# Square roots by a power operation on GpSimd, and small vector chains moved from VectorE to GpSimd

## The chip, the cores and the metric

The kernel runs on one core of a Trainium2 chip. A core has a matrix engine (TensorE, PE in the profile), a vector engine (VectorE, DVE), a scalar engine (ScalarE, ACT), a general engine (GpSimd, POOL) and an engine that mostly issues transfers (SyncE, SP). Each works through its own queue of instructions in order, and semaphores tie the queues together. The metric is device microseconds of one execution; lower is better.

## The reference, cut to what matters

Two layers work on x (8 batches of 112 rows by 256) with a context of 8 x 375 x 256. All arithmetic is float32.

```python
x = x + L0_xattn(layernorm(x), ctx)           # 16 heads of 16, biases
x = x + L0_ffn(layernorm(x))                  # routed, 8 experts, best 2
x = x + L1_xattn(layernorm(x), ctx, mask)     # additive mask
x = x + L1_ffn(layernorm(x))                  # quantized to ternary weights, depthwise conv, silu
```

with

```python
layernorm(x)  = (x - mean) / sqrt(var + 1e-5)
project(v)    = v * min(1, 0.95 / |v|)                      # into a ball
x_hyper = project(x @ Wp + bp);  c = project(centroids)     # 8 centroids
diff  = max(|x_hyper|^2 + |c|^2 - 2 x_hyper.c, 0)
denom = (1 - |x_hyper|^2)(1 - |c|^2) + 1e-7
dist  = arccosh(max(1 + 2 diff / denom, 1 + 1e-7))
top 2 of -dist, softmax of the two as weights
out   = sum over the two of weight * (gelu(x @ W1[e] + b1[e]) @ W2[e] + b2[e])
```

Square roots are needed in three places: 1/sqrt(var + eps) of each normalization (one number a row), 0.95/|v| of the ball (one number a row, eight for the centroids), and sqrt(m*m - 1) in the softmax of two arccosh values (two numbers a row).

## The kernel before, in words

The eight batches are the unit of work; a tile of one batch has 112 partitions (rows of x) by 256 columns. The program has four stages one after the other.

The first attention (0 to about 297 us) carries a routing pipeline inside it. A plan lists the steps of every batch with a slot (four slots a batch) and a place in the slot: normalize and transpose (`norm`, `t_n`), query, key and value products (`t_q`, `t_k`, `t_v`), scores and their row maxima (`sc`, `top`, L587), the scores turned round with the maximum folded in (`t_p`), exponentials on ScalarE (`pT`), the weighted values (`po`), and the closing steps, of which `project` adds into x and takes the statistics of the new x (`ln_stats`). From slot 4b+13 on come the eight routing steps of batch b: `norm` (writes `rn`) and `turn` (`t_rn`), `hyper` (`t_xh`), `centre` (g, the ball's scale r), `distance` (v), two `pick`s, `place` and `weigh`. `place` works out the row in the scratch tensor `tok` to which each token goes (`at`) and issues two scatters of `rn` from GpSimd's queue (L375). A scatter waits until the one before it has landed, since both write `tok`. `rn` has two buffers, so the normalized row of batch b+2 waits until both scatters of batch b are through. `weigh` works out the two shares. The plan gives the order of priority; the framework then schedules the instructions of each engine by its own cost estimates and sets the semaphores.

The expert stage (297 to 456 us) runs 21 tiles of 128 tokens through the experts' weights, which stream in by transfers from SP's queue; it begins with a load of `tn` from `tok`. The second attention (456 to 701 us) starts each batch with `combine`: two gathers from GpSimd's queue (L510), two weighted additions into x on VectorE (L514), and statistics. Then it is the first attention again, with a mask and without routing: VectorE adds the mask to `pT` (L627). The last stage (701 to 793 us) quantizes, convolves and multiplies, and is mostly VectorE's.

`rsqrt` (L184 to L202) makes a first guess from the exponent bits by a shift and a multiply-add on integers, and improves it by three Newton steps, all on VectorE: nine instructions for one number a row, eleven for more. `ln_stats` (L204), `ball_scale` (L255) and `weigh` (L383) call it. `ln_apply` (L215, its instruction on L217) does the normalization proper, also on VectorE.

Of the kernel before, what the change touches and what calls it, by code (L numbers as in the profile page):

```python
# [54 lines left out]
def xattn_ffn_kernel(  # L55
# [129 lines left out]
    def rsqrt(x, dst, n, name):  # L185


        p = x.shape[0]
        h = sp.tile([p, n], F32, tag=f"{name}h", name="h")
        a = sp.tile([p, n], F32, tag=f"{name}a", name="a")  # L190
        bits = dst.bitcast(I32)
        nc.vector.tensor_scalar(bits, x.bitcast(I32), 1, None, ALU.logical_shift_right)
        nc.vector.tensor_scalar(bits, bits, -1.0, 1597463007.0, ALU.mult, ALU.add)
        if n == 1:
            nc.vector.tensor_scalar_mul(h, x, -0.5)
        for _ in range(3):
            if n == 1:
                nc.vector.scalar_tensor_tensor(a, dst, dst, h, ALU.mult, ALU.mult)  # L198
            else:
                nc.vector.tensor_mul(a, dst, dst)  # L200
                nc.vector.scalar_tensor_tensor(a, a, -0.5, x, ALU.mult, ALU.mult)
            nc.vector.scalar_tensor_tensor(dst, a, 1.5, dst, ALU.add, ALU.mult)  # L202

    def ln_stats(b):  # L204

        st = sp.tile([S, 6], F32, tag="bnst", name="bnst")
        nc.vector.bn_stats(st, xs[b])
        mv = sp.tile([S, 2], F32, tag=f"mv{b}", name="mv")
        nc.vector.bn_aggr(mv, st)
        nc.vector.tensor_scalar_add(mv[:, 1:2], mv[:, 1:2], 1e-5)  # L210
        rs = sp.tile([S, 1], F32, tag=f"rs{b}", name="rs")
        rsqrt(mv[:, 1:2], rs, 1, "ln")
        return mv, rs

    def ln_apply(dst, b, stats):  # L215
        mv, rs = stats
        nc.vector.tensor_scalar(dst, xs[b], mv[:, 0:1], rs, ALU.subtract, ALU.mult)  # L217
# [28 lines left out]
    class Router:  # L246
# [9 lines left out]
        def ball_scale(self, sq, r, n, name):  # L256

            c = self.tmp(f"c{name}", n, sq.shape[0])
            nc.vector.tensor_scalar_max(c, sq, 1e-14)
            rsqrt(c, r, n, f"ball{name}")  # L260
            nc.vector.tensor_scalar(r, r, 0.95, 1.0, ALU.mult, ALU.min)

        def centroids(self):
# [9 lines left out]
            self.ball_scale(self.cn, cs, E, "c")  # L273
# [6 lines left out]
        def norm(self, b, stats):  # L280
            n = self.pool.tile([S, D], F32, tag="r_n", name="rn")
            ln_apply(n, b, stats)
# [25 lines left out]
        def centre(self, xh, xsq):  # L308
# [9 lines left out]
            self.ball_scale(g[:, E : E + 1], r, 1, "x")  # L318
            return g, r

        def distance(self, g, r):

            tmp = self.tmp
            xn = tmp("xn", 1)
            nc.vector.scalar_tensor_tensor(xn, g[:, E : E + 1], r, r, ALU.mult, ALU.mult)
            nc.vector.tensor_scalar_min(xn, xn, 0.99)
            xn1 = tmp("xn1", 1)
            nc.vector.tensor_scalar(xn1, xn, -1.0, 1.0, ALU.mult, ALU.add)
            m2r = tmp("m2r", 1)
            nc.vector.tensor_scalar_mul(m2r, r, -2.0)  # L330

            dif = tmp("dif", E)
            nc.vector.scalar_tensor_tensor(dif, g[:, 0:E], m2r, self.cn[:S], ALU.mult, ALU.add)
            nc.vector.tensor_scalar(dif, dif, xn, 0.0, ALU.add, ALU.max)

            den = tmp("den", E)
            nc.vector.tensor_scalar(den, self.cn1[:S], xn1, 1e-7, ALU.mult, ALU.add)
            nc.vector.reciprocal(den, den)
            nc.vector.scalar_tensor_tensor(dif, dif, 2.0, den, ALU.mult, ALU.mult)
            nc.vector.tensor_scalar(dif, dif, 1.0, 1.0 + 1e-7, ALU.add, ALU.max)  # L340
            v = tmp("v", E)
            nc.vector.tensor_scalar_mul(v, dif, -1.0)
# [17 lines left out]
        def place(self, b, n, ohs):  # L360
# [9 lines left out]
            for k in range(2):  # L370
                nc.vector.tensor_mul(sel[:, k], ohs[k], row)
            nc.vector.tensor_reduce(rf, sel, AX.X, ALU.add)
            nc.vector.tensor_copy(at[b], rf)
# [654 lines left out]
```

## Time and profile before

| | |
|---|---|
| median of 3 runs | 796.31 us (794.44 to 800.98) |
| the profiled execution | 795.12 us, span 793.4 us |
| mean granted PE clock | 0.841 |
| busy: PE, DVE, ACT, POOL | 670.2, 462.1, 240.9, 43.3 us |
| instructions: PE, DVE, POOL | 5906, 1664, 83 |
| DVE rows of the Newton steps on one number of a normalization (L198, L202) | 96 of 219 ns, 96 of 157 ns |
| two-input addition on POOL, 112x256 (L521) | 8 of 726 ns |
| scatter and gather issues on POOL (L375, L510) | 16 of 954 ns, 16 of 937 ns |

A row of the profile names a line of the kernel, the engine, the operation, what is written and read, the shapes, how often, and the busy time with the mean of one. The time after the bar is how long the engine stood idle just before such instructions, and what ended that. A row in order of time begins with its start and its length in us.

### The profile page before, as it was taken

How to read it: one execution, taken by the hardware profiler on the slowest of the kernel's cores; microseconds unless marked ns; L12 is line 12 of the kernel's file. 1: busy time of each engine (PE TensorE's matmuls, PEld its weight loads, DVE VectorE, ACT ScalarE, POOL GpSimd, SP SyncE). 2: the span in 40 equal slices, each digit the busy share in tenths (PEclk: the TensorE clock that was granted, in tenths of full speed). 3: DMA queues.
4: the chain of work that ended last, by engine and by line, in shares of the span. 5: the costliest groups of instructions: out<-in, count | busy, mean ns of one | idle time of the engine just before them, and what ended most of it. 6: DMA issues, size and time to landing. Idle time of an engine off the chain costs nothing.

```text
span 793.4 us, 15060 instructions
## 1 busy us (share of the span) xinstructions
PE 670.2 (84%) x5906; PEld 483.3 (61%) x5906; DVE 462.1 (58%) x1664; ACT 240.9 (30%) x476; POOL 43.3 (5%) x83
## 2 busy tenths in 40 slices
PE   4999998999989819999999968999999989845143
PEld 2666666666656519998999844566666656621033
DVE  8853767766844760111111148759887785569975
ACT  1123342323233204434334310133433322317300
POOL 4000000100000110000000061000000000000000
PEclk9998999989777959999999975579999985556558
DMA  9999101002000115988899420000000000000001
GB/s 309 366 344 321 62 2 54 14 13 68 14 12 8 31 45 206 332 287 327 331 351 344 169 82 19 1 2 1 2 2 2 2 2 1 1 1 0 0 11 35
DMA packets 37074, 82.73 MB, mean 104 GB/s; under 512 B 3228, under 2 KB 29196, under 8 KB 31628
## 3 DMA queue, kind: packets, MB, share of 16 engines
q1 hardware_dynamic: 34092, 76.25, 27.2%
q0 software_dynamic: 1536, 3.67, 1.5%
q10 hardware_dynamic: 1376, 1.87, 0.7%
q8 instruction: 46, 0.75, 0.4%
q14 instruction: 24, 0.20, 0.1%
HBM read 61.59 MB, written 20.19 MB: 103 GB/s over the span
## 4 chain that ended last, share of the span: by engine, by line
PE 68%; DVE 20%; DMA 5%; issue 4%; ACT 3%; POOL 0%; another core or an unknown queue 0%; POOLq 0%; DVEq 0%; ACTq 0%; SPq 0%
PE t_k L229 10%; PE t_h L799 10%; PE t_y L810 9%; PE t_p L617 8%; PE sc L584 7%; PE po L639 6%; PE t_q L534 4%; PE t_v L236 4%; DMA tok<-rn,at 2%; DVE a L198 2%; PE t_out L672 2%; DVE am L924 2%; PE t_o L651 1%; DVE top L587 1%; PE t_y L942 1%
## 5 line engine op out<-in xcount | busy, mean ns | idle before, releaser
L229 PE MATMUL t_k<-ctx,wk 128*128 128x375 f32 x256 | 100.5, 538 | 4.0 <-DMA ctx<-in_ctxT_dram 3.2
L799 PE MATMUL t_h<-tnT,we 128*128 128x128 f32 x672 | 91.4, 280 | 0.6 <-DMA we<-in_WA_dram 0.4
L799 PEld LDWEIGHTS t_h<-tnT,we 128*128 128x128 f32 x672 | 87.1, 193 | 7.5 <-ACT hT L803 1.6
L584 PE MATMUL sc<-k,q 16*112 16x375 f32 x512 | 88.0, 593 | 4.3 <-DVE pT L627 3.2
L803 ACT ACTIVATE hT<-t_h,we 128x128 f32<-128x128 f32 x168 | 61.4, 368 | 91.3 <-PE t_h L799 85.7
L617 PE MATMUL t_p<-qa,k 17*125 17x112 f32 x1536 | 81.9, 323 | 2.4 <-DVE top L587 1.5
L810 PE MATMUL t_y<-we,hT 128*128 128x256 f32 x336 | 82.8, 380 | 0.0
L629 ACT ACTIVATE pT<-pT 125x672 f32<-125x672 f32 x64 | 48.8, 763 | 107.7 <-DVE pT L627 105.5
L617 PEld LDWEIGHTS t_p<-qa,k 17*125 17x125 f32 x1536 | 65.0, 215 | 21.2 <-issue 14.8
L587 DVE TENSOR_REDUCE top<-sc 112x2 f32<-112x750 f32 x64 | 57.9, 935 | 27.2 <-PE sc L584 27.2
L229 PEld LDWEIGHTS t_k<-ctx,wk 128*128 128x128 f32 x256 | 51.1, 211 | 37.1 <-issue 9.7
L627 DVE TENSOR_TENSOR pT<-t_p,maskT 125x336 f32<-125x336 f32 x128 | 56.6, 500 | 24.9 <-PE t_p L617 24.9
L639 PE MATMUL po<-pT,v 125*32 125x112 f32 x1536 | 65.9, 299 | 6.1 <-ACT pT L629 3.7
L629 ACT ACTIVATE pT<-t_p 125x672 f32<-125x672 f32 x64 | 43.3, 728 | 90.7 <-PE t_p L617 90.7
L594 DVE CUSTOM_DVE_ANT_0 sm<-sc,mask 112x375 f32<-112x375 f32 x128 | 63.1, 543 | 9.9 <-PE sc L584 9.9
L639 PEld LDWEIGHTS po<-pT,v 125*32 125x32 f32 x1536 | 43.4, 124 | 31.4 <-ACT pT L629 13.3
L810 PEld LDWEIGHTS t_y<-we,hT 128*128 128x128 f32 x336 | 59.1, 191 | 5.5
L788 DVE COPY tnT<-t_tn 128x256 f32<-128x256 f32 x21 | 8.9, 425 | 77.2 <-PE t_tn L786 70.6
L812 DVE TENSOR_TENSOR y<-t_y,we 128x256 f32<-128x256 f32 x21 | 8.9, 425 | 68.9 <-PE t_y L810 63.9
L584 PEld LDWEIGHTS sc<-k,q 16*112 16x112 f32 x512 | 29.4, 192 | 30.9 <-issue 19.7
L236 PE MATMUL t_v<-wv,ctx 128*125 128x256 f32 x192 | 45.9, 387 | 0.3 <-ACT k L557 0.3
L534 PEld LDWEIGHTS t_q<-nT,wq 128*128 128x128 f32 x256 | 36.2, 225 | 7.5 <-DVE qa L607 3.7
(207 smaller groups left out, 780.6 us busy)
## 6 DMA issues: line engine op xcount, KB each, us to landing
we<-in_WB_dram SPq DMA_DIRECT2D x21, 1152.0 KB, 8.2
we<-in_WA_dram SPq DMA_DIRECT2D x21, 1028.0 KB, 6.5
tok<-zero SPq DMA_DIRECT2D x8, 896.0 KB, 9.7
ysc<-zero SPq DMA_DIRECT2D x8, 896.0 KB, 10.8
ctx<-in_ctxT_dram SPq DMA_DIRECT2D x8, 375.0 KB, 6.5
tn<-tok SPq DMA_DIRECT2D x21, 128.0 KB, 7.4
ysc<-y SPq DMA_DIRECT2D x21, 128.0 KB, 3.3
we<-in_w1T_dram SPq DMA_DIRECT2D x1, 1024.0 KB, 9.4
```

The lines of the kernel that those rows point to most:

```text
L229: nc.tensor.matmul(t, wts[layer]["k"][:, c, g * 128 : (g + 1) * 128], ctx_t[b][:, c, :], start=(c == 0), stop=(c == 1),)
L236: nc.tensor.matmul(t, ctx_t[b][:, c, i * KC : (i + 1) * KC], wts[layer]["v"][:, c, :], start=(c == 0), stop=(c == 1),)
L534: nc.tensor.matmul(t[:, g, :], wts[layer]["q"][:, c, g * 128 : (g + 1) * 128], nT[:, c, :], start=(c == 0), stop=(c == 1),)
L584: nc.tensor.matmul(ts[j // 2][:S, j % 2, :SK], q[r, g, :], k[r, g, :], start=True, stop=True)
L587: nc.vector.tensor_reduce(top[:, g, 2 * m : 2 * m + 2, A : A + 1], ts[m][:S, :, :SK], AX.X, ALU.max, negate=True,)
L594: nc.vector.tensor_tensor_reduce(out=sm, in0=ts[m][:S, i, :SK], in1=mask_t, scale=-1.0, scalar=3.0e38, op0=ALU.add, op1=ALU.min, accum_out ...
L617: nc.tensor.matmul(ts[j // 2][:KC, j % 2, c * S : (c + 1) * S], k[r, g, c * KC : (c + 1) * KC], qa[r, g, :], start=True, stop=True,)
L629: nc.scalar.activation(pT, src, AF.Exp)
L639: nc.tensor.matmul(po[32 * j : 32 * j + 32, g, :], v[:, c, 4 * g + j, :], pTs[j // 2][:, j % 2, c * S : (c + 1) * S], start=(c == 0), stop ...
L799: nc.tensor.matmul(ph[:, i, :], w1[:, c, f * 128 : (f + 1) * 128], nt[:, c, :], start=(c == 0), stop=(c == 1),)
L803: nc.scalar.activation(hT[:, f, :], ph[:, i, :], AF.Gelu, bias=b1[:, f : f + 1])
L810: nc.tensor.matmul(py, hT[:, f, :], w2[:, f, :], start=(f == 0), stop=(f == NF - 1))
```

## The change

`rsqrt` becomes a single GpSimd instruction that raises to the power -0.5, with a constant tile of -0.5 as its second operand. The addition of 1e-5, the scaling of the ball, the whole of `distance` but its reciprocal, the two selections, the integer copy and the running count of `place`, and `weigh` but its reciprocal go to GpSimd with it. So do the routing normalization, and the attentions' normalization of every batch but the first. Where an instruction of VectorE took three operands (a tensor, a column and a second tensor), GpSimd has two instructions in its place. `distance` is put in another order.

```diff
-    def rsqrt(x, dst, n, name):
-        p = x.shape[0]
-        h = sp.tile([p, n], F32, tag=f"{name}h", name="h")
-        a = sp.tile([p, n], F32, tag=f"{name}a", name="a")
-        bits = dst.bitcast(I32)
-        nc.vector.tensor_scalar(bits, x.bitcast(I32), 1, None, ALU.logical_shift_right)
-        nc.vector.tensor_scalar(bits, bits, -1.0, 1597463007.0, ALU.mult, ALU.add)
-        if n == 1:
-            nc.vector.tensor_scalar_mul(h, x, -0.5)
-        for _ in range(3):
...
+    minus_half = const([128, E], "mhalf")
+    nc.gpsimd.memset(minus_half, -0.5)
+
+    def rsqrt(x, dst):
+        nc.gpsimd.tensor_tensor(dst, x, minus_half[: x.shape[0], : x.shape[1]], ALU.pow)
 
     def ln_stats(b):
...
-        nc.vector.tensor_scalar_add(mv[:, 1:2], mv[:, 1:2], 1e-5)
         rs = sp.tile([S, 1], F32, tag=f"rs{b}", name="rs")
-        rsqrt(mv[:, 1:2], rs, 1, "ln")
+        nc.gpsimd.tensor_scalar_add(rs, mv[:, 1:2], 1e-5)
+        rsqrt(rs, rs)
         return mv, rs
 
-    def ln_apply(dst, b, stats):
+    def ln_apply(dst, b, stats, eng=None):
         mv, rs = stats
-        nc.vector.tensor_scalar(dst, xs[b], mv[:, 0:1], rs, ALU.subtract, ALU.mult)
+        (eng or nc.vector).tensor_scalar(dst, xs[b], mv[:, 0:1], rs, ALU.subtract, ALU.mult)
...
         def distance(self, g, r):
...
+            tmp, eng = self.tmp, nc.gpsimd
+            xn, xn1, m2r = tmp("xn", 1), tmp("xn1", 1), tmp("m2r", 1)
+            eng.tensor_scalar(m2r, r, -2.0, None, ALU.mult)
+
+            dif, den = tmp("dif", E), tmp("den", E)
+            eng.tensor_scalar(dif, g[:, 0:E], m2r, None, ALU.mult)
+            eng.tensor_scalar(xn, g[:, E : E + 1], r, r, ALU.mult, ALU.mult)
+            eng.tensor_scalar(xn, xn, 0.99, None, ALU.min)
+            eng.tensor_scalar(xn1, xn, -1.0, 1.0, ALU.mult, ALU.add)
+
+            eng.tensor_scalar(den, self.cn1[:S], xn1, 1e-7, ALU.mult, ALU.add)
             nc.vector.reciprocal(den, den)
+            eng.tensor_add(dif, dif, self.cn[:S])
+            eng.tensor_scalar(dif, dif, xn, 0.0, ALU.add, ALU.max)
+            eng.tensor_mul(dif, dif, den)
+            eng.tensor_scalar(dif, dif, 2.0, 1.0, ALU.mult, ALU.add)
             v = tmp("v", E)
+            eng.tensor_scalar(v, dif, 1.0 + 1e-7, -1.0, ALU.max, ALU.mult)
             return v
...
             for k in range(2):
-                nc.vector.tensor_mul(sel[:, k], ohs[k], row)
+                nc.gpsimd.tensor_mul(sel[:, k], ohs[k], row)
             nc.vector.tensor_reduce(rf, sel, AX.X, ALU.add)
-            nc.vector.tensor_copy(at[b], rf)
+            nc.gpsimd.tensor_copy(at[b], rf)
...
+            nc.gpsimd.tensor_scalar(z, m, 1.0, None, ALU.add)
+            nc.gpsimd.tensor_scalar(q, m, -1.0, None, ALU.add)
+            nc.gpsimd.tensor_mul(z, z, q)
+            rsqrt(z, q)
+            nc.gpsimd.tensor_mul(q, q, z)
+            nc.gpsimd.tensor_sub(u, q, m)
+            nc.gpsimd.tensor_add(r, u[:, 0:1], u[:, 1:2])
             nc.vector.reciprocal(r, r)
+            nc.gpsimd.tensor_scalar(share[b][:, 0:1], u[:, 1:2], r, None, ALU.mult)
+            nc.gpsimd.tensor_scalar(share[b][:, 1:2], u[:, 0:1], r, None, ALU.mult)
...
-                ln_apply(n, b, stats.pop(b))
+                ln_apply(n, b, stats.pop(b), nc.gpsimd if b else nc.vector)
```

## The prediction

> **What bounds the kernel now.** I read the page's busy shares first, then busy time by stretch, then the chain of work that ended last, then single instructions in order of time where TensorE (PE) stood still.
>
> ```profile
> PE 670.2 (84%) x5906; PEld 483.3 (61%) x5906; DVE 462.1 (58%) x1664; ACT 240.9 (30%) x476; POOL 43.3 (5%) x83
> ...
> PE 68%; DVE 20%; DMA 5%; issue 4%; ACT 3%; POOL 0%; another core or an unknown queue 0%; POOLq 0%; DVEq 0%; ACTq 0%; SPq 0%
> ```
>
> PE carries 68% of the chain, VectorE (DVE) 20%, GpSimd (POOL) nothing. An average hides the stages, so here they are (columns: stretch; PE, weight loads, DVE, ACT, POOL busy; granted PE clock; DMA share; GB/s):
>
> ```profile
> 100.00:230.00 130.00, 122.44 (x1335) 84.64 (x1328) 85.80 (x361) 43.19 (x88) 6.55 (x7) 0.87 0.08 25
> 230.00:264.00 34.00, 28.84 (x331) 19.49 (x330) 19.09 (x132) 10.83 (x20) 3.77 (x4) 0.85 0.05 15
> 264.00:297.00 33.00, 15.91 (x85) 12.14 (x83) 22.86 (x174) 4.42 (x12) 5.66 (x6) 0.72 0.13 41
> ...
> 505.00:640.00 135.00, 134.87 (x1531) 87.54 (x1529) 106.29 (x371) 48.09 (x70) 0.00 (x0) 0.93 0.01 2
> 640.00:701.00 61.00, 53.89 (x521) 34.36 (x519) 33.55 (x114) 16.57 (x25) 0.00 (x0) 0.56 0.01 1
> ```
>
> In 100:230 (first attention, with routing) PE is nearly full but not always at full clock; 264:297 is a routing tail in which PE mostly waits; in 640:701 PE is busy at half clock. The waits inside:
>
> ```profile
> 230.43 0.94 POOL L375 DMA_INDIRECT tok<-rn,at  x1 [27.24 <-DVE cx L259]
> 234.07 0.94 POOL L375 DMA_INDIRECT tok<-rn,at  x1 [2.70 <-DMA tok<-rn,at]
> 236.68 0.41 DVE L217 TENSOR_SCALAR rn<-x,mv,rs 112x256 f32<-112x256 f32 x1 [1.30 <-DMA tok<-rn,at]
> 237.24 0.38 PE L288 MATMUL t_rn<-ident,rn 112*128 112x112 f32 x2 [1.43 <-DVE oh L349]
> ...
> 288.38 0.94 POOL L375 DMA_INDIRECT tok<-rn,at  x1 [4.80 <-DVE q L202]
> ...
> 471.08 0.64 PE L524 MATMUL t_n<-ident,n 112*128 112x112 f32 x2 [7.07 <-DVE rs L202]
> ...
> 643.98 0.16 DVE L202 SCALAR_TENSOR_TENSOR rs<-a,rs 112x1 f32<-112x1 f32 x1
> 644.06 1.75 DVE L627 TENSOR_TENSOR pT<-t_p,maskT 125x336 f32<-125x336 f32 x4
> 645.13 0.89 PE L584 MATMUL sc<-k,q 16*112 16x375 f32 x4 [1.62 <-DVE pT L627]
> ```
>
> The second scatter waits for the first to land, the normalized row `rn` two batches on waits for both (two buffers), and PE's `t_rn` waits for `rn`. At 644 us a root on DVE (642.3 to 644.1) holds `pT` up, PE stands 1.62 us, and its clock falls to half.
>
> **What the skill says.** (1) GPSIMD Engine Reference, § 3.1 Elementwise: a two-input f32 add of 2048 columns takes 4497 ns on GpSimd. The trace's only such row is L521, 256 columns, 726 ns; together a slope of 2.1 ns per column and a fixed part of 726 - 256 x 2.1 = 190 ns. The select of masks.py:199 (128 columns, 288 ns), at the memset slope of L157 (1369 / 1536 = 0.9), leaves 177 ns: they agree. (2) Same page, § 2.1 Instruction dispatch: the first call of a freshly loaded GpSimd routine may cost about 6 us; no run here shows it. (3) SBUF — State Buffer, § Who interferes with whom: a DVE instruction with two SBUF inputs blocks against a GpSimd instruction that reads; GpSimd is too idle before to show it. (4) TensorE: Matmul & The Clock Gate, Part 1: an idle window of about 3.4 us halves the clock, and a busy one restores it. The trace agrees on the drop after the 7.07 us gap, but at 644 us it dropped after less, and stayed at 0.50 to 712 us through stretches of full PE: partly.
>
> **The change, part by part.**
>
> *DVE gets lighter.* Per routed batch 55 DVE instructions go: variance and its root 10 (1.68 us busy), ball scale 11 (1.86), distances 10 (1.84), weights 18 (2.96), placing 4 (0.59), the two normalizations 2 (0.87): 9.8 us, from rows such as L198, 20.2 us for 96. Over the kernel, with 24 more roots and the centroids, about 124 of 462 us. The reciprocals, picks and PSUM copies stay.
>
> *POOL gets it.* A small dependent operation: 0.19 us from (1) plus about 0.05 for the semaphore, T = 0.24 us (low 0.2; high 0.45, should two pointer operands cost a second fixed part). The power P is shown nowhere: at least 0.2, as any two-input operation; above, no page prices it, and I take 2.2, the price at which it decides (below). I take 0.5. A 256-column normalization lies between 0.4 (memset slope) and 0.73 (L521): 0.5. A routed batch then costs POOL 26 x 0.24 + 3 x 0.5 + 2 x 0.5 + 0.73 + two scatters at 0.95 = 11.4 us, and some 5 us of blocked waits, of a 29 us period: it fits, so POOL matters by latency and order, not load.
>
> *Start, 0:17 us: nothing.* PE begins when the context lands at 11.38 us, and its first keys run to 17.05; `t_n` waited 0.24 us. The roots now queue behind the memsets (ended 7.85) and all eight variances, so the first power ends near 12 us. Without that cover, with a 6 us first call, +1.3 us.
>
> *First attention, 100:230: -9.* A routed batch takes 29.3 us (t_k at 96.7, 126.0, 154.6, 184.6). In the second attention it takes 24.1 (529.7, 553.9, 578.1) with the same PE work less the router's 2.9 us (t_xh 1.0, the two transposes, g, rank), so PE's floor is 27.0. 4.5 batches x 2.3 = 10.4; the chain has 26 us of DVE in this stretch, enough to cover it. I take 9: `recip den` and the picks now block DVE behind POOL, with large maxima (L587) queued behind them.
>
> *Routing tail, 230:297: +8.5.* On POOL the changed program has, in order: first scatter of batch b, all 14 operations of the distances of b+1, second scatter, the weights of b+1 (which need its picks), then `rn` of b+2. From `at` at 230.0: scatter to 231.2, distances 13 T + P + 0.3 for DVE's reciprocal = 3.9, the next root 0.74, so v at 235.9; second pick's maximum 1.3 later (six small DVE operations); weights 6 T + P + 0.3 + 2 T = 2.7; count 0.24; `rn` ends about 240.7, not 237.1: +3.6. The next batch likewise (254.0 to 261.5 before): +3.0. At the end: g of the last batch at 279.4, but POOL is free only at 281.0 (weights, place and scatter of the one before); v at 285.9 (before 283.6); pick, rank; then its weights, which now stand ahead of its place, so its first scatter starts at 291.7, not 288.4: +3.3. Together 9.9, less 1.4 of PE waits on DVE and ACT in this stretch that go.
>
> *Second attention's entry: -2.* POOL has nine gathers (1.25 us apart from 458.79) ahead of the first addition of 1e-5, and a tenth ahead of the first power: gather nine ends 469.7, addition 469.95, gather ten and its gap to 471.2, power 471.7, `n` 472.4 against 471.0: +1.3. But `q` no longer stands behind the second root and `n` (477.07): t_q ends 477.2, sc starts 477.9, not 479.78: -1.9.
>
> *Second attention: -1 in 505:640 (of 4.4 us DVE on the chain there), -6.6 in 640:701:* 1.6 for the wait at 645, and 5 for the clock. 640:701 had 53.9 us of busy PE at 0.56; warm throughout it would save some 20. I credit a quarter, since the thin last batches leave gaps anyway.
>
> *Last stage: -0.8:* the last root's ten issue slots (0.06 to 0.13 us each) between 702.6 and 707 leave DVE's queue; quantizing stays there.
>
> *Contention (3): 0.* Each meeting costs at most one small operation, and DVE has slack where POOL is busy; uncovered, +2.
>
> Sum: -9 + 8.5 - 2 - 1 - 6.6 - 0.8 = -10.9. The profiled run took 795.1 (span 793.4 and 1.7 around it), giving 784.2; the median of the runs is 1.2 higher: 785.
>
> **Rivals.**
> *The clock does not follow.* Half-clock stretches come as before: take 4 off the first stretch's gain (its share at clock 0.87) and 5 off the second's: 794. For: the clock stayed down through full PE. Against: its trigger at 644 us was a DVE root.
> *DVE's stalls were what cooled PE.* Clock 0.87 over 130 us means 34 us at half, some 16 us lost; recovering that instead of 9, and 15 instead of 5 later, gives 768. For: dips at 210 to 228 us follow a 1.16 us wait on DVE. Against: the longer waits for `rn` cool PE too.
> *POOL's latency becomes the bound (slower).* About 100 POOL operations and 11 powers lie on the tail's path. T = 0.35 adds 11, P = 1.7 adds 13: 809. It is slower by 1% from T = 0.44 alone, or P = 2.2 alone. For: no small reading operation and no power appears in the trace. Against: two rows give the same fixed part.
>
> **How the numbers follow.** Forecast 785 (778 to 791): 0.38; clock does not follow, 794: 0.21; clock held, 768: 0.18; POOL-bound, 809: 0.23. 1% is 8 us, about what a measurement of this kernel tells from no change. Faster: 0.18 and five sixths of 0.38, 0.50; slower 0.23; within 1% the rest, 0.27. The low end, 766, covers the held clock; the high end, 808, cuts POOL-bound in about half.
>
> **What would show it.** Right: DVE near 340 us busy, POOL near 130; `rn` ending four us later after `at` in the tail; t_k spaced about 27 us from 100 to 200; the wait of sc at 645 gone, the clock above 0.56 behind it. Wrong: powers over 1 us, small POOL rows over 0.35, DVE idle before `den`, or `t_rn` waiting for POOL before 200 us.

## The result and the profile after

The changed kernel takes 822.07 us (median of 4 runs, 819.56 to 828.9), 1.0327 times the kernel before, with a 95% interval of 1.025 to 1.0405. It is some 26 us slower; the forecast was 785 us, with a range up to 808.

The busy shares and the chain of work that ended last, from the page of the changed kernel:

```profile
PE 681.9 (83%) x5906; PEld 492.3 (60%) x5906; DVE 382.8 (47%) x965; ACT 241.0 (29%) x476; POOL 156.7 (19%) x389
...
PE 69%; DVE 12%; POOL 8%; DMA 5%; issue 4%; ACT 2%; SPq 0%; DVEq 0%; POOLq 0%; ACTq 0%
```

DVE lost 699 instructions and 79.3 us of busy time, and its share of the chain fell from 20% to 12%. POOL, which had no share before, now carries 8%. What was taken from one chain has come back on another, and longer.

Where it came back is read between landmarks that both kernels have: the addition into x that closes a batch of the first attention (`x<-t_out`, first batch b0 to last b7), and the first transpose of the expert stage (`t_tn`), with which the routing tail ends.

| stretch | before | after | difference |
|---|---|---|---|
| start to b0 | 88.4 | 84.2 | -4.2 |
| b0 to b5 | 142.1 | 153.3 | +11.2 |
| b5 to `t_tn`, the routing tail | 65.5 | 88.4 | +22.9 |
| `t_tn` to the end of the span | 497.4 | 492.0 | -5.4 |
| span | 793.4 | 817.9 | +24.5 |

The first two rows vary by themselves. Three kernels below have the first attention exactly as before; with the kernel before they give 85.2 to 88.4 us for the first row, 142.1 to 147.9 (mean 145.6) for the second, 65.1 to 67.1 for the third. So of the second row some 7 us are the change; of the third, nearly all.

Busy time by stretch after (columns: stretch and its length; PE, weight loads, DVE, ACT, POOL busy; granted PE clock; DMA share; GB/s): the first periods, the tail, four periods of the second attention, and its end.

```profile
100.00:230.00 130.00, 122.86 (x1236) 82.67 (x1236) 57.66 (x137) 39.11 (x81) 44.01 (x125) 0.78 0.08 25
237.50:325.80 88.30, 50.34 (x408) 36.31 (x405) 20.09 (x97) 15.15 (x32) 44.20 (x127) 0.69 0.07 20
571.00:664.00 93.00, 92.87 (x1134) 61.75 (x1133) 73.23 (x228) 35.48 (x51) 7.22 (x14) 1.00 0.01 2
664.20:724.00 59.80, 54.66 (x521) 35.44 (x520) 29.52 (x85) 17.13 (x25) 2.37 (x6) 0.53 0.01 1
```

The same tail, four periods and end in the kernel before, between the same landmarks:

```profile
230.50:296.00 65.50, 43.29 (x408) 30.81 (x400) 41.28 (x300) 15.25 (x32) 9.36 (x10) 0.79 0.09 27
543.00:639.50 96.50, 96.36 (x1135) 63.01 (x1135) 80.86 (x291) 35.53 (x52) 0.00 (x0) 1.00 0.01 2
639.50:699.00 59.50, 52.55 (x521) 33.94 (x520) 33.93 (x115) 17.07 (x25) 0.00 (x0) 0.57 0.01 1
```

In the tail the same 408 matmul records take 7 us more of busy PE, at a granted clock of 0.69 and no longer 0.79, and PE stands still 38 us instead of 22. In 100:230 PE is as busy as before (122.9 and 122.4 us), but at 0.78 instead of 0.87. That is so in this one execution; the experiments below show what of it repeats.

The tail, instruction by instruction, in order of time (start, length, and in brackets the wait ahead of it and what ended it):

```profile
237.12 1.09 POOL L360 DMA_INDIRECT tok<-rn,at  x1 [0.29 <-POOL at L358]
241.49 0.20 DVE L321 RECIPROCAL den<-den 112x8 f32<-112x8 f32 x1 [3.12 <-POOL den L320]
243.50 0.16 DVE L333 TENSOR_REDUCE m<-v 112x1 f32<-112x8 f32 x1 [1.76 <-POOL v L327]
243.63 1.10 POOL L360 DMA_INDIRECT tok<-rn,at  x1 [0.17 <-issue]
247.27 0.17 DVE L381 RECIPROCAL su<-su 112x1 f32<-112x1 f32 x1 [1.76 <-POOL su L380]
247.41 0.62 DVE L593 TENSOR_TENSOR qa<-t_top,q 128x448 f32<-128x448 f32 x1
248.08 1.19 PE L603 MATMUL t_p<-qa,k 17*125 17x112 f32 x16 [6.80 <-DVE qa L593]
248.27 1.25 POOL L205 TENSOR_SCALAR rn<-x,mv,rs 112x256 f32<-112x256 f32 x1
279.24 0.64 PE L275 MATMUL t_rn<-ident,rn 112*128 112x112 f32 x2 [6.04 <-POOL rn L205]
315.46 0.54 PE L349 MATMUL po<-ind,below 112*112 112x8 f32 x2 [10.70 <-DVE ind L343]
325.87 1.09 PE L772 MATMUL t_tn<-ident,tn 128*128 128x128 f32 x4 [8.57 <-DMA tn<-tok]
```

The order on POOL is the predicted one: first scatter at 237.12, distances, second scatter at 243.63, weights, `rn` at 248.27. What the prediction didn't follow is DVE's order. Its reciprocal of the denominators, the picks and the reciprocal of the weights stand ahead of `qa` in DVE's queue, and wait for POOL; so PE waits 6.8 us for a `qa` that has nothing to do with routing. One batch on, PE waits 6.04 us for `rn`, with key products and the last batch's closing steps behind it; at the end 10.7 us for `ind`, which itself stands behind the reciprocal of the weights.

Over the first attention and the tail (84:326) DVE stands still for POOL in front of these two reciprocals, eight times each (total, times, longest one):

```profile
DVE su L381 <- POOL su L380: 24.3, 8, 4.2
DVE den L321 <- POOL den L320: 23.1, 8, 4.5
```

In the kernel before, where DVE works the whole chain out by itself, it stood 0.2 us before the one and not at all before the other.

PE's longest waits in the tail, with total, times and longest one, of the changed kernel:

```profile
PE t_rn L275 <- POOL rn L205: 10.7, 2, 6.0
PE po L349 <- DVE ind L343: 10.7, 1, 10.7
...
PE t_p L603 <- DVE qa L593: 6.8, 1, 6.8
```

and of the kernel before:

```profile
PE po L364 <- DVE ind L358: 7.6, 2, 6.8
PE t_rn L288 <- DVE rn L217: 1.5, 1, 1.5
PE t_rn L288 <- DVE oh L349: 1.4, 1, 1.4
...
PE t_p L617 <- DVE qa L607: 0.7, 1, 0.7
```

POOL's groups by shape (name, shapes, count; busy us, mean ns; idle before), where the costs can be held against those forecast:

```profile
L190 POOL TENSOR_TENSOR rs<-rs,mhalf 112x1 f32<-112x1 f32 x32 | 18.1, 571 | 1.8
L205 POOL TENSOR_SCALAR n<-x,mv,rs 112x256 f32<-112x256 f32 x14 | 17.6, 1256 | 94.5 <-PE t_n L510 93.9
...
L190 POOL TENSOR_TENSOR q<-z,mhalf 112x2 f32<-112x2 f32 x8 | 5.8, 726 | 0.6
...
L316 POOL TENSOR_SCALAR xn<-g,r 112x1 f32<-112x1 f32 x8 | 2.7, 343 | 0.0
...
L190 POOL TENSOR_TENSOR cs<-cs,mhalf 128x8 f32<-128x8 f32 x1 | 1.6, 1647 | 0.0
```

The power was forecast well (0.5 us, measured 0.57 for one column and 0.73 for two). The small operations last 0.19 to 0.35 us and follow one another at 0.28 to 0.35 us when one needs the other; forecast 0.24. The 256-column normalization lasts 1.25 us, not 0.5, three times what it took on DVE (0.41).

### The profile page after: what moved, and what is told of

Same layout as the page of the kernel before. It is cut to its first block, busy times and chain, and to the rows that moved or that the text cites. A ratio compares the mean times of both kernels' runs of the same rounds, so it can differ in the third digit from the quotient of the medians.

```text
span 817.9 us, 14700 instructions
## 1 busy us (share of the span) xinstructions
PE 681.9 (83%) x5906; PEld 492.3 (60%) x5906; DVE 382.8 (47%) x965; ACT 241.0 (29%) x476; POOL 156.7 (19%) x389
## 4 chain that ended last, share of the span: by engine, by line
PE 69%; DVE 12%; POOL 8%; DMA 5%; issue 4%; ACT 2%; SPq 0%; DVEq 0%; POOLq 0%; ACTq 0%
PE t_k L217 10%; PE t_h L785 9%; PE t_y L796 8%; PE t_p L603 8%; PE sc L570 7%; PE po L625 6%; PE t_v L224 5%; PE t_q L520 4%; PE t_out L658 2%; DVE am L910 2%; PE t_o L637 1%; DMA tok<-rn,at 1%; DVE y L899 1%; PE t_y L928 1%; PE t_xh L284 1%
## 5 line engine op out<-in xcount | busy, mean ns | idle before, releaser
L217 PE MATMUL t_k<-ctx,wk 128*128 128x375 f32 x256 | 105.6, 560 | 4.5 <-DMA ctx<-in_ctxT_dram 3.8
L603 PE MATMUL t_p<-qa,k 17*125 17x112 f32 x1536 | 85.7, 335 | 11.2 <-DVE qa L593 8.4
L603 PEld LDWEIGHTS t_p<-qa,k 17*125 17x125 f32 x1536 | 68.0, 226 | 30.6 <-issue 15.2
L217 PEld LDWEIGHTS t_k<-ctx,wk 128*128 128x128 f32 x256 | 53.4, 221 | 39.4 <-issue 12.5
L580 DVE CUSTOM_DVE_ANT_0 sm<-sc,mask 112x375 f32<-112x375 f32 x128 | 62.6, 542 | 11.2 <-PE sc L570 11.1
L224 PE MATMUL t_v<-wv,ctx 128*125 128x256 f32 x192 | 48.8, 400 | 0.3 <-ACT k L543 0.3
L496 POOL DMA_INDIRECT yg<-ysc,at x16 | 15.5, 969 | 171.5 <-issue 170.7
L199 POOL TENSOR_SCALAR rs<-mv 112x1 f32<-112x1 f32 x32 | 7.8, 246 | 180.4 <-DVE mv L197 179.8
```

Source lines behind the costliest of these rows:

```text
L217: nc.tensor.matmul(t, wts[layer]["k"][:, c, g * 128 : (g + 1) * 128], ctx_t[b][:, c, :], start=(c == 0), stop=(c == 1),)
L224: nc.tensor.matmul(t, ctx_t[b][:, c, i * KC : (i + 1) * KC], wts[layer]["v"][:, c, :], start=(c == 0), stop=(c == 1),)
L580: nc.vector.tensor_tensor_reduce(out=sm, in0=ts[m][:S, i, :SK], in1=mask_t, scale=-1.0, scalar=3.0e38, op0=ALU.add, op1=ALU.min, accum_out ...
L603: nc.tensor.matmul(ts[j // 2][:KC, j % 2, c * S : (c + 1) * S], k[r, g, c * KC : (c + 1) * KC], qa[r, g, :], start=True, stop=True,)
```

## The experiments

The kernels below carry both forms of every chain, so their line numbers differ from those above. Their landmarks, from one profiled execution each, and the ratio to the kernel before with its 95% interval. The kernel before, taken beside the experiments, had medians from 794.4 to 798.5 us, so kernels are compared by the ratio and not by their times:

| kernel | b0 to b5 | b5 to `t_tn` | `t_tn` to end | ratio |
|---|---|---|---|---|
| before | 142.1 | 65.5 | 497.4 | 1 |
| changed | 153.3 | 88.4 | 492.0 | 1.0327 [1.025, 1.0405] |
| second_half | 147.3 | 67.1 | 489.9 | 0.9917 [0.9889, 0.9946] |
| first_half | 152.2 | 86.5 | 497.5 | 1.0366 [1.0313, 1.0418] |
| dist_back | 148.3 | 73.4 | 494.0 | 1.0104 [1.0044, 1.0165] |
| weigh_back | 148.6 | 81.5 | 492.5 | 1.0189 [1.0153, 1.0224] |
| rn_back | 148.7 | 85.4 | 491.5 | 1.0230 [1.0163, 1.0297] |
| su_pow | 147.3 | 89.0 | 491.5 | 1.0241 [1.0207, 1.0274] |
| recips_pow | 159.6 | 93.1 | 490.9 | 1.0402 [1.0366, 1.0439] |
| rn_bufs | 151.9 | 89.2 | 492.3 | 1.0267 [1.0224, 1.0311] |
| late_dve | 152.1 | 65.6 | 491.8 | 1.0042 [1.0018, 1.0066] |
| early_dve | 141.6 | 86.7 | 491.2 | 1.0182 [1.0148, 1.0215] |
| roots_only | 145.1 | 69.7 | 494.2 | 1.0058 [1.0019, 1.0097] |
| route_dve | 149.8 | 65.1 | 491.8 | 0.9983 [0.9956, 1.001] |
| no_newton | 141.4 | 61.1 | 498.4 | 0.9895 [0.9844, 0.9946] |
| second_roots | 145.0 | 66.5 | 497.3 | 0.9990 [0.9969, 1.001] |
| second_norms | 147.9 | 65.1 | 495.2 | 1.0002 [0.9974, 1.0031] |

**The two halves.** Against the changed kernel, second_half leaves the first attention and the routing as before and moves only the roots of the second attention's and the last stage's normalizations, and the second attention's normalizations but the first. first_half is the complement.

```diff
-            ln_apply(n, b, stats, nc.gpsimd)
+            ln_apply(n, b, stats)
...
-                ln_apply(n, b, stats.pop(b), nc.gpsimd if b else nc.vector)
+                ln_apply(n, b, stats.pop(b), nc.gpsimd if b and ("v", "p")[layer] == "p" else nc.vector)
...
-                stats_next[b] = ln_stats(b)
+                stats_next[b] = ln_stats(b, ("v", "p")[layer])
```

Here `"v"` stands for VectorE and `"p"` for GpSimd, and `layer` is 0 in the first attention and 1 in the second. `ball_scale`, `distance`, `place` and `weigh` are those of the kernel before.

> Only the second attention and the last stage are changed: their roots by the power on GpSimd and their normalizations there; the first attention with its routing is as before. Theory (all of the loss arises in the first attention, since the changed kernel's first expert transpose starts at 325.9 us and not 296.05, and the 492.0 us from there to the end are 5.4 less than before): about 791 us, expert stage starting at 296. Rival (the changed first attention, or clock luck, sets what comes after): no gain, 796, or a loss.

> The complement: start, first attention and routing as in the changed kernel, second attention and last stage as before. Theory: 796 + 30 = 826 us, the expert stage starting at 326. Rival: the two halves don't add; then it lies at 815 or below.

Measured: 791.94 us, 0.9917; and 825.73 us, 1.0366. The second half gains 6 to 7 us, the first loses 28 to 29, and the two add up, within their intervals, to the whole (1.0283 against 1.0327). Both theories held: the whole loss is made before `t_tn`.

**Routing's parts, back on VectorE one at a time.** Each is the changed kernel with one chain as before: ball and distances (dist_back), weights (weigh_back), the normalization `rn` (rn_back). su_pow leaves the weights on GpSimd and takes their reciprocal there too.

dist_back has `ball_scale` and `distance` of the kernel before, weigh_back its `weigh`, rn_back `ln_apply(n, b, stats)` in `norm`; su_pow:

```diff
-            nc.vector.reciprocal(r, r)
+            nc.gpsimd.tensor_tensor(r, r, minus_one[:S], ALU.pow)
```

> The changed kernel with the ball's scale of x and the distances wholly on VectorE with the Newton root, as before. On GpSimd they took 4.7 us from g to v (140.5 to 145.0 in the changed kernel), ahead of the second scatter, the next root and the normalized row, and VectorE stood 2 to 4.6 us a batch for the reciprocal in their middle. Blocked queue and long path: 10 to 14 us faster than the changed kernel, 808 to 812, with TensorE's waits for rn and ind in the tail (13 and 9 us in all) falling by half. If the parts add, weights (9.4 measured) and distances make up most of the 26 us. Rival (the clock, or the shared port): within 3 us.

> The changed kernel with the weights wholly on VectorE with the Newton root, as before. Blocked queue: as the power of -1, plus 18 VectorE instructions of 0.16 us back, 808 to 814. Long path: GpSimd's queue loses some 3.5 us a batch ahead of the normalized row and of the last places, so also faster, by 8 to 12 us. Both agree here; it parts from the power of -1 by how much more it brings: nothing more if the queue blocks, all of it if the path is long.

> The changed kernel with the routing normalization on VectorE. It saves GpSimd 1.25 us a batch, costs VectorE 0.41, and takes rn out of GpSimd's queue behind the weights; but the root before it and the second scatter stay there. Long path: 4 to 8 us faster, 814 to 818, and TensorE's wait for rn in the tail shrinks. Blocked queue: nothing, or slower, since VectorE now waits for the scatter as well.

> The changed kernel, but the reciprocal in the weights is a power of -1 on GpSimd in place of a reciprocal on VectorE, so VectorE no longer stands in line for GpSimd in the middle of the weights (3.6 to 4.2 us a batch in the changed kernel, with the sum of query and maximum and the row maxima queued behind it). Theory of the blocked queue: 8 to 14 us faster than the changed kernel, 808 to 814, and TensorE's wait of 6.8 us for that sum in the tail goes. Rival of the long path (GpSimd's latency on the way to the normalized row and to the places): the weights' chain is the same length, so no more than 3 us.

Measured: 801.94, 812.66, 811.91 and 816.83 us. The first and the third ran where the kernel before took 794.4 us, the other two where it took 798.1; by the ratios the four gain 2.2%, 1.4%, 1.0% and 0.9% on the changed kernel (18, 11, 8 and 7 us), though only the first two lie clear of its interval. In the tail, against 88.4: 73.4 with the distances back, 81.5 with the weights, 85.4 with `rn`. Their gains sum to 25 us, about what the tail lost. The order is plain: the chain of distances, thirteen operations and a power between `g` and the first pick, weighs most, more than was expected of it. With it back on DVE, PE waits 0.7 us for `qa` in the tail, as in the kernel before, and no longer 6.8.

su_pow takes one hand-over to DVE away. The wait of `su` is gone, PE's wait for `qa` in the tail falls from 6.8 to 5.0 us, that for `rn` rises from 10.7 to 13.1, and the tail is as long as it was (89.0): there the long path is right. What it gained, less than the blocked queue foretold and more than the long path, was gained before the tail: 147.3 us from b0 to b5, as in kernels with the first attention of before. That is one execution, and what it shows of the hand-over in the steady stretch stays open.

**Hand-over or length of the chain.** recips_pow takes both of DVE's reciprocals out of POOL's chains.

```diff
-            nc.vector.reciprocal(den, den)
+            eng.tensor_tensor(den, den, minus_one[:S], ALU.pow)
-            nc.vector.reciprocal(r, r)
+            nc.gpsimd.tensor_tensor(r, r, minus_one[:S, 0:1], ALU.pow)
```

> The changed kernel with both reciprocals, of the distances and of the weights, as powers of -1 on GpSimd, so that VectorE no longer stands in the middle of a GpSimd chain. If VectorE blocked in the middle, with large maxima and scores behind it, is most of the tail's loss: TensorE's wait for qa (8.4 us) goes, the first expert transpose comes at 316 to 319 us instead of 325.9, the whole is 809 to 813. If the length of GpSimd's chain is it: the eight-column power (1.65 us) stands for 0.6 us of hand-over, about 1 us more a batch than su_pow (816.8), the transpose comes at 323 to 327, the whole is 816 to 822.

Measured: 831.81 us, beyond both expectations. Its interval overlaps that of the changed kernel, but not those of su_pow and of rn_bufs (below; it ran beside this one and took 821.01). In its tail, DVE's wait for the distances and PE's for `qa`:

```profile
254.31 0.16 DVE L365 TENSOR_REDUCE m<-v 112x1 f32<-112x8 f32 x1 [6.55 <-POOL v L359]
...
257.11 1.61 PE L635 MATMUL t_p<-qa,k 17*125 17x112 f32 x24 [6.66 <-DVE qa L625]
```

With no reciprocal between, the first pick waits for the whole chain in one piece, and `qa` behind it waits as long as before (6.66, not 6.80). So doing away with the hand-overs doesn't help: the chain as a whole is too long, and any instruction of DVE that needs its end holds up what stands behind. The run also makes the chain longer (eight columns of power, 1.67 us here), and that costs more: from b0 to b5, where it takes 159.6 us, PE waits 11.0 us for row maxima `top` that stand in DVE's queue.

**The place of `rn`.** rn_bufs gives the routing normalization four buffers; it waits for no scatter any more and stands ahead of the weights in POOL's queue.

```diff
-            n = self.pool.tile([S, D], F32, tag="r_n", name="rn")
+            n = self.pool.tile([S, D], F32, tag=f"r_n{b % 2}", name="rn")
```

> The changed kernel with four buffers instead of two for the routing normalization, which then waits for no scatter and stands ahead of the weights in GpSimd's queue. If the place of rn in that queue is a good part of the tail's loss: TensorE's waits for rn fall from 10.7 us to under 5, the transpose comes at 317 to 320 us, the whole is 810 to 815. If the loss is the chain of distances alone: 819 to 823.

Measured: 821.01 us, in the range for the chain alone. (By the ratio, 1.0267, it lies some 5 us under the changed kernel and between the two expectations, but the intervals overlap.) PE's waits in its tail:

```profile
PE po L379 <- DVE ind L373: 14.2, 2, 10.7
...
PE t_p L633 <- DVE qa L623: 8.1, 1, 8.1
PE t_rn L305 <- POOL rn L228: 6.1, 2, 4.6
```

The wait for `rn` fell from 10.7 to 6.1 us, those for `ind` and `qa` rose from 10.7 to 14.2 and from 6.8 to 8.1. One wait took the place of another, and the tail is as long (89.2).

**Which batches.** In late_dve GpSimd routes batches 0 to 3 and VectorE batches 4 to 7; early_dve is the other way round (`b >= 4` in the diff). The rest is the changed kernel.

```diff
+    def on_gpsimd(b):
+        return b < 4
...
-                        r["v"] = rt.distance(*r.pop("g"))
+                        r["v"] = (rt.distance if on_gpsimd(b) else rt.distance_v)(*r.pop("g"))
```

> The changed kernel in which GpSimd routes batches 0 to 3 only; batches 4 to 7 (ball, distances, places, weights, routing normalization and its root) are VectorE's, as before. If the loss sits in the routing tail, where the last batches' chains follow one another: the first expert transpose comes at 298 to 306 us and the whole is 0.992 to 1.002 of the time before. If half of it sits in the four periods before: 1.010 or more.

> The complement: VectorE routes batches 0 to 3, GpSimd batches 4 to 7. If the loss sits in the routing tail: 1.025 to 1.035, the first expert transpose at 320 to 327 us. If half of it sits in the four periods before: 1.010 to 1.020.

Measured: 1.0042 and 1.0182, late_dve a little above the range for a loss that is all in the tail, early_dve in the range for half. Both have the second half's gain, so they are read against 0.9917: batches 0 to 3 on GpSimd cost 1.25%, 10 us, batches 4 to 7 cost 2.65%, 21 us, and the two together (31) are about what the changed kernel loses against second_half (4.1%, 33). The landmarks agree: late_dve has the tail of before (65.6) and 152.1 ahead of it, early_dve 141.6 and a tail of 86.7. So two thirds of the loss are the tail's and a third is made before it, where the prediction saw a gain. PE's waits in the tail of early_dve, then of late_dve:

```profile
PE po L409 <- DVE ind L403: 10.7, 1, 10.7
PE t_rn L308 <- POOL rn L231: 10.6, 2, 6.0
...
PE t_p L702 <- DVE qa L692: 7.0, 1, 7.0
```

```profile
PE po L433 <- DVE ind L403: 7.6, 2, 6.8
PE t_rn L308 <- DVE rn L231: 1.1, 1, 1.1
...
PE t_p L702 <- DVE qa L692: 0.7, 1, 0.7
```

early_dve has the waits of the changed kernel, late_dve those of the kernel before. The granted clock goes with them: 0.68 or 0.69 in the tails of the changed kernel, first_half, early_dve and rn_bufs, and 0.76 to 0.81 in every kernel whose tail has the waits of before.

**What the first four batches lose.** From b0 to b5, in order before, second_norms (whose first attention is that of before), changed, first_half (whose first attention is that of the changed kernel) and late_dve:

```profile
88.40:230.50 142.10, 134.54 (x1464) 92.84 (x1466) 92.36 (x383) 47.97 (x95) 6.62 (x8) 0.88 0.08 25
85.20:233.10 147.90, 143.02 (x1489) 97.14 (x1485) 92.57 (x384) 47.92 (x95) 6.73 (x8) 0.82 0.08 25
84.20:237.50 153.30, 145.82 (x1459) 98.38 (x1462) 64.59 (x153) 47.97 (x95) 46.98 (x132) 0.80 0.07 23
87.60:239.80 152.20, 140.48 (x1462) 95.40 (x1466) 64.38 (x153) 47.93 (x95) 46.90 (x132) 0.83 0.07 24
87.80:239.90 152.10, 140.07 (x1461) 95.08 (x1464) 65.57 (x167) 47.92 (x95) 44.67 (x129) 0.84 0.07 23
```

PE stands still 7.6 and 4.9 us in the first two, 7.5 in the changed kernel, but 11.7 and 12.0 in first_half and late_dve, with a clock no lower than that of second_norms. PE's waits there in first_half:

```profile
PE t_p L633 <- DVE qa L623: 2.8, 1, 2.8
PE t_p L633 <- DVE top L603: 2.4, 1, 2.4
PE t_q L550 <- DVE qa L623: 1.7, 2, 1.1
```

They are those of the tail, only shorter: `qa` and `top` stand in DVE's queue behind the two reciprocals. In late_dve the reciprocal of the weights waits 4.16 us for POOL and `qa` starts behind it, while PE waits.

**Does VectorE's load bound the first attention?** roots_only moves the first attention's roots alone (of the normalizations, the ball of x and the weights), from the kernel before. route_dve is the changed kernel with all of routing back on VectorE, but for the roots of the normalizations: these and the attention's normalizations stay on GpSimd in both attentions. no_newton is the kernel before without the Newton steps of the first attention.

The core of roots_only (ball and weights likewise):

```diff
-            nc.vector.tensor_scalar_add(mv[:, 1:2], mv[:, 1:2], 1e-5)
-            rsqrt(mv[:, 1:2], rs, 1, "ln")
+            nc.gpsimd.tensor_scalar_add(rs, mv[:, 1:2], 1e-5)
+            rsqrt(rs, rs)
```

and of no_newton, where `steps[0]` is 0 in the first attention and 3 from then on:

```diff
-        for _ in range(3):
+        for _ in range(steps[0]):
```

> The kernel before, with only the roots of the first attention (normalizations, ball of x, weights) as powers on GpSimd; every chain and normalization stays on VectorE. If the power itself (0.57 us for one column, 0.73 for two, each with two crossings of about 0.15) is harmless, 790 to 800 against 797 for the kernel before: three crossings a batch against 29 VectorE instructions less. If any wait of VectorE for GpSimd costs, 803 or more.

> The changed kernel with ball, distances, places, weights and the routing normalization on VectorE with Newton roots; on GpSimd stay the roots of all normalizations (with the addition of 1e-5) and the normalizations of every batch but the first, in both attentions. These have some 7 us or more between their result and its use. Theory: faster than the kernel before by the 6 us of the second half and 0 to 6 more in the first attention, 784 to 791. Rival (any small operation on GpSimd in the first attention costs): 792 to 800.

> The kernel before with the Newton steps of every root in the first attention left out (its roots are then first guesses, good to some 3%): VectorE loses some 17 us between 100 and 230 us and GpSimd gets nothing. Read from the second to the sixth addition into x, 116.3 us in the kernel before and 120.1 in second_half. If VectorE's load set this stretch, as the prediction had it, it falls to 107 to 111, and the whole to some 780 us. If TensorE's own work at its granted clock sets it, it stays at 116 to 120; only the routing tail behind it gets shorter, by 2 to 3 us for each of the last batches, and the whole is 786 to 790 us.

Measured: 798.72 us (1.0058), 793.4 (0.9983) and 790.23 (0.9895). The first 100 to 230 us of no_newton:

```profile
100.00:230.00 130.00, 122.90 (x1384) 84.41 (x1384) 77.95 (x291) 43.44 (x88) 7.48 (x8) 0.88 0.08 25
```

From the second to the sixth addition into x no_newton takes 114.0 us, between the two expectations and nearer to the second, at whose end the whole lies too; the kernels with an unchanged first attention take 116.3, 119.1, 120.1 and 120.5. With nothing in their place, leaving the Newton steps out of this stretch is worth 2 to 6.5 us in these single executions, and not 9. But it takes less work from DVE than the change does: the busy column fell by 7.9 us (17 had been expected) and in the changed kernel by 28. roots_only carries 71.1 us of DVE from 100 to 230 us instead of 85.8 and takes 118.4 us from the second to the sixth addition. As a whole it is slower than the kernel before by 0.6%, 4 to 5 us, and its interval leaves out 1: it lies between its two expectations, with a tail of 69.7 us. route_dve missed its expectation of a gain and lies in the rival's range: its second attention gained 5.6 us against the profiled run of before, its first gained nothing.

**Which part of the second half gains.**

second_roots is second_half with

```diff
-                ln_apply(n, b, stats.pop(b), nc.gpsimd if b and ("v", "p")[layer] == "p" else nc.vector)
+                ln_apply(n, b, stats.pop(b), nc.gpsimd if b and ("v", "v")[layer] == "p" else nc.vector)
```

so that every normalization is VectorE's again, and second_norms is second_half with the Newton steps of before in `ln_stats`.

> The kernel before with the second attention's roots (and the last stage's) on GpSimd, its normalizations back on VectorE; the first attention as before. second_half, with both moved, had 0.9917 of the time before. If the roots bring it: 0.990 to 0.994. If moving the 256-column normalizations off VectorE brings it: 0.997 to 1.001. If the normalization on GpSimd (1.25 us against 0.41) costs latency there: below 0.990.

> The kernel before with the second attention's normalizations of all batches but the first on GpSimd, their roots still Newton steps on VectorE; the first attention as before. If the normalizations carry the gain of second_half (0.9917) by themselves: 0.989 to 0.995, the attention's period 23.4 us instead of 24.2. If it needs both: 0.997 to 1.001.

Measured: 0.999 and 1.0002. By its figure second_roots answered "the normalizations", and second_norms then took that answer back: neither part gains alone, both together gain 0.8%. The times between the closing products (`t_out`) of the batches say why in part. second_norms has the period of before, 24.2 us. second_roots has 23.35 us in one of the four periods after the first, as second_half has in all four (23.35 to 23.5), but 24.7 to 24.9 in the other three, two of them with a dip of 3.4 us to half the clock (at 572 and 620 us). Such a dip costs 1.7 us of full clock, about what these two are longer. So the roots can shorten the period, and while the normalization is still DVE's most of that is lost again. What causes the dips stays open. That both together gain doesn't rest on second_half alone: from `t_tn` to the end the eleven kernels that move both take 489.9 to 494.0 us, the others 494.2 to 498.4.

The best kernel here is second_half, 0.9917 of the time before. no_newton is below it only because it leaves work out.

## Why the prediction was wrong

**"First attention, 100:230: -9" is the first step that failed, in its sign.** It compared the period of 29.3 us with the second attention's 24.1 plus the router's products, and took the 2.3 us between for waits on DVE. The page had the waits, and the prediction didn't ask for them. In the kernel before, PE's waits for DVE in these 130 us are:

```profile
PE po L639 <- DVE w1mean L455: 2.2, 1, 2.2
...
PE t_p L617 <- DVE top L587: 1.2, 1, 1.2
PE t_q L534 <- DVE qa L607: 1.1, 2, 0.7
```

That is 4.5 us, half of what was to be gained, and 2.2 of it (`w1mean`) is work that the change doesn't touch. Time of DVE on the chain, which the prediction took as cover for its gain, is not time that PE waits. A difference in the clock, 0.87 here against 1.00 in the periods that it was compared with (543:639.5), would be enough for the rest: 0.13 of a period is 3.8 us, more than the 2.3. no_newton, with some of DVE's load gone and nothing in its place, gained 2 to 6.5 us.

With POOL in the chain the stretch from b0 to b5 became some 7 us longer instead, and late_dve and early_dve put 10 us on the first four batches. Where that goes can't be read from the changed kernel's profile alone. In it PE waits no more than before and the clock is lower, but in first_half, with the same first attention, PE stands still 4 us longer and has a higher clock than in the changed kernel. Four kernels have the first attention of before: from b0 to b5 PE stands still 4.9 to 7.6 us in them, at 0.82 to 0.88. The changed kernel and three others that route these batches on GpSimd (first_half, late_dve, rn_bufs) have 7.5 to 12.0 us, at 0.80 to 0.85. On average they take 6.8 us more, and 4.2 of it is PE standing still. So more than half is DVE's queue held up behind POOL, the very thing for which the prediction took 1.4 us off its gain; the rest is the lower clock, and as that varies by as much between executions of one code, its cause is not shown.

**"Routing tail: +8.5" had the right mechanism and less than half its size.** It measured +22.9 (some 21 against kernels with the same first attention). Its parts were predicted as 3.6, 3.0 and 3.3, less 1.4; from b5 to b6, b6 to b7 and b7 to `t_tn` they are 6.1, 9.5 and 7.2. Three things made the sum short. T was 0.28 to 0.35 us instead of 0.24: from `r` at 238.25 to v at 243.47 the chain takes 5.2 us, not 4.7 (3.9 and the next root's 0.74). `rn` took 1.25 us instead of 0.5. Both together put the end of `rn` 12.9 us behind `at`, where 10.7 was forecast and 7.1 was the case before. The third is a wait that the sum doesn't have: the prediction followed only POOL's own chain. It wrote that "`recip den` and the picks now block DVE behind POOL, with large maxima (L587) queued behind them", but charged it, and too little, to the first attention alone; in the tail `qa` stood there, and PE with it, for 6.8 us. 16 us of the tail are longer waits of PE, and 7 the lower clock that goes with them. That moving the distances alone back to DVE takes 15 of the 23 us away, and late_dve all of them, shows that POOL's chains are the cause.

**The costs of operations.** The power: right. T: 0.24 taken, 0.28 to 0.35 measured, inside its range (0.2 to 0.45) and close to the 0.35 at which the rival put 11 us. The normalization: 1.25 us against a range that ended at 0.73. The range was made from an addition of two tensors; this operation, with two steps and two column operands, is slower than that, and no row of before showed it. (In the fixed part, 288 - 128 x 0.89 is 174 ns and not 177; nothing hangs on it.) The first call's 6 us (GPSIMD Engine Reference, § 2.1) didn't show, as taken: no power of one column lasted over 0.69 us, the first included.

**"POOL matters by latency and order, not load"**: right. It was busy 156.7 us (forecast near 130) and idle for the rest, and the kernel was slower all the same.

**Second half: -10.4 forecast, -5.4 measured, right in sign.** Entry -2: the first closing product comes 244.96 us after `t_tn` instead of 246.85, -1.9, but this landmark lies far behind the steps that were forecast. Counted from the first gather, the first `t_n` comes 1.3 us later, as forecast, and the first `sc` 1.2 us sooner, not 1.9: the mechanism is right and a little too large, and that the later landmark shows the very figure is luck. "-1 in 505:640": four periods took 93.4 instead of 96.6 us, -3.2, more than forecast, although PE was booked as 99.9% busy there before: part of a full PE's time must be waiting that the page doesn't separate. "-6.6 in 640:701": nothing, 59.4 against 59.3. The wait of `sc` for `pT` at 645 is gone, as forecast, but the clock fell all the same, so the rival that the clock does not follow was right on this stretch. At half clock it stood from 647 to 716 us before, from 671 to 739 after, from 646 to 714 in second_half: 68 us each, the last batches' thin work and the start of the last stage included, with the root on DVE or not. That root was not the trigger. Last stage -0.8: -0.4.

**Start and contention, nothing each.** b0 came at 84.2 us, a little ahead of the 85.2 to 88.4 of the kernels with the start of before, but at 87.6 in first_half, whose start is the changed one. DVE's weighted additions into x, with two inputs in SBUF, last 474 ns, and 477 before; its selections `oh` among POOL's chains 224, and 226 before: no cost of contention, as taken.

**The rivals.** "POOL's latency becomes the bound" was what happened, and its price was wrong: its 809 us added 11 us for T = 0.35, which nearly came about, and 13 for powers of 1.7 us, which did not. What carries the time from the forecast of 785 to 822 is the first attention (from -9 to +7, 16 us), the tail (from 8.5 to 21 or 23, some 13) and the second half (from -10.4 to -5.4, 5): 819. The point from which that rival was to decide, T = 0.44 for 1%, was too high because it stood on top of the 9 us that never were to be had. "The clock does not follow" was right as to the clock and took nothing else into account. By the signs listed beforehand, DVE near 340 us was missed (382.8: added up one by one, DVE's durations fell by 126 us, close to the forecast of 124, but busy time, in which durations that overlap count once, fell by 79), `t_k` stands 31 to 33 us apart and not 27, DVE idle before `den` came, `t_rn` waiting for POOL came but not before 200 us, and powers over 1 us came only for eight columns.

## What to carry to other kernels

Before crediting a lighter engine with a faster stage, add up the bound engine's waits for it in that stage; a period compared with another stage's must be compared at the same granted clock. Before reading a change of a few us from one profile, read a second execution of the same code. A chain of small dependent operations moved to a slower engine costs the sum of its start-to-start times where batches follow one another closely, and it also holds up every queue in which something waits for its end: list what stands behind that instruction, in the tail as well as in the steady stretch. Where only a root and one normalization move, and nobody waits for them soon (here the second attention), the same move gains 0.8%, if both move.

## What the runs showed that was not expected

- A normalization of 112x256 with two column operands takes 1.25 us on GpSimd, 0.41 on VectorE, and 0.73 is what an addition of two such tensors takes on GpSimd. The Trainium skill (GPSIMD Engine Reference, § 4.1 Engine selection) puts GpSimd at about half VectorE's speed for operations of two inputs and says that "1-input is roughly line-rate"; here, with one tensor as input, it is a factor of three.
- A power on GpSimd takes 0.57, 0.73 and 1.65 us for one, two and eight columns: about 0.15 us for each column more.
- Once down near the end of the second attention, PE's clock stayed at half for 68 us in most kernels, and up to 75 in the others. In the kernel before, the changed one and second_half PE was 79% busy meanwhile, and over 90% in the first 52 us of it. The page TensorE: Matmul & The Clock Gate, Part 1, lets a busy window of about 3.4 us restore it. Elsewhere in these runs dips end after 3.4 us (in second_roots at 572 and 620 us); here the clock didn't come back.
- Executions with an identical first attention differ by up to 6 us in it (142.1 to 147.9 from b0 to b5), with clocks of 0.88 to 0.82. A landmark of one execution is good to a few us.
